# A recurrent graph kernel: gates and updates as a pinned pipeline of half batches, the first half batch's gate products inside the last product chain, and one set of sums in another order

## The chip, the cores and the metric

The kernel runs on one core of one Trainium2 chip. The metric is the device time of an execution in microseconds (us); lower is better. Quoted times are medians of several executions. Every execution in this study was in the fast state, at a granted TensorE clock of 0.995 to 0.999 of full speed.

## The reference, cut to what matters

A batch of 16 graphs with 1024 nodes and 128 features shares one dense 1024 x 1024 matrix `adj`. The first layer is one product with `adj`, a residual and a layer norm. The second is a gated recurrence of five steps, in which both the "in" and the "out" matrix are `adj`:

```python
def step(h, _):
    m_in = jnp.einsum('nm,bmd->bnd', in_matrix, h)      # in_matrix == out_matrix == adj
    m_out = jnp.einsum('nm,bmd->bnd', out_matrix, h)
    av = jnp.concatenate([m_in, m_out], axis=-1)
    u3 = h @ u3_w.T + u3_b
    z = jax.nn.sigmoid(av @ w3_w.T + w3_b + u3)
    r = jax.nn.sigmoid(av @ w4_w.T + w4_b + u3)
    hv = jnp.tanh(av @ w5_w.T + w5_b + (r * h @ u5_w.T + u5_b))
    h = (1.0 - z) * h + z * hv
    return (h, None)
# layer 0: x = layernorm(x + adj @ (x @ weight) + bias)
# layer 1: x = layernorm(x + five steps of the above on x)
```

## The kernel before

The product with `adj` (an **aggregation**) takes four batches at once, a group, so there are 4 aggregations for the first layer and 4 x 5 = 20 for the second. In this text they are numbered 0 to 23, and a **step** is the stretch from one aggregation's start to the next one's: aggregation, then gates and updates of four batches. In 12 of the steps, here called closing steps (10 to 13, 15 to 18 and 20 to 23), the group before is normalised and stored as well; steps without that are called plain. An aggregation is a two-level Strassen-Winograd scheme: outer products 1 to 7, each of them built from seven inner products, called P1 to P7 here. They run as four chains, for the outer pairs (1,2), (3), (6,7) and (5,4). Inputs of the inner products are sums that VectorE makes: four "outer sums" (`tsum`, 1.22 us each) and "inner sums" (`inner`). The inner products share three banks of PSUM:

```python
        after = {
            1: lambda: nc.scalar.copy(fb, fa),            # P1 is copied into pb, on which P6, P7, P4 accumulate
            5: lambda: nc.scalar.copy(x22, fc),
            6: lambda: nc.scalar.copy(x12, fb),
            2: lambda: nc.scalar.copy(x11, fa),
            7: lambda: nc.vector.tensor_add(x22, fb, x22),  # reads pb; P4 may not write it before
            3: lambda: nc.vector.tensor_add(x12, fc, x12),
            4: lambda: nc.scalar.copy(x21, fb),
        }
        bank_of = {1: pa, 2: pa, 5: pc, 3: pc, 6: pb, 7: pb, 4: pb}
        for a in order:
            for hook in hooks.get(a, ()):
                hook()
            for o, n in enumerate(ns):
                for c in range(2):
                    product = nc.tensor.matmul(bank_of[a][:, ts(o, QT)], chunk(a, o, c), left[n][a][:, c, :], ...)
            ...
            with tc.high_priority(), behind:
                after[a]()
            drain(3 if len(ns) == 2 else 1)      # a few activations of a deferred normalisation
```

The gates work on half batches of 512 columns, eight to a step. Each takes five products: the first one by `u3`, then `w4` (for r) and `w3` (for z), then the two update products by `w5` and `u5`. The first product is used twice: `w4` accumulates on top of it in its own bank, and ScalarE copies it to a second bank (`seeded`) for `w3`. I call that copy the seed copy.

```python
    def gate_first(tag, k, h):
        pu = bank(f"pu_{tag}_{k}_{h}")                    # one of three rotating banks, taken as they come free
        pin(nc.tensor.matmul(pu, w_t["u3"], hid[:, k, ts(h, HALF)], start=True, stop=True, ...))
        pin(nc.scalar.copy(seeded[h], pu))
        pus[h] = pu

    def gate_rest(tag, k, h):
        ...
        pin(nc.tensor.matmul(pu, w_t["w4"], agg[:, k, cols], start=False, stop=True, ...))
        pin(nc.scalar.activation(rh[:, cols], pu, AF.Sigmoid, bias=br))
        pin(nc.vector.tensor_mul(rh[:, cols], rh[:, cols], hid[:, k, cols]))
        pin(nc.tensor.matmul(pz, w_t["w3"], agg[:, k, cols], start=False, stop=True, ...))
        pin(nc.scalar.activation(z[:, cols], pz, AF.Sigmoid, bias=bz))
...
            hooks[54][4] = [call(gate_half, tag, 0, 0)]   # ahead of P4 of the last chain
            aggregate(tag, rows, hooks, s > 0)
            gate_half(tag, 0, 1)
            for k in range(QUAD):
                if k < QUAD - 1:
                    gates(tag, k + 1)
                update(tag, k, not last)
```

`pin` pins nothing in the steps: it calls `keep_in_program_order` only near the end of the program. What is not pinned is ordered by the framework's scheduler when the program is built. `keep_in_program_order` keeps an instruction behind whatever the program text has pinned before it on the same engine.

## Time and profile before

| | before |
|---|---|
| time, median of the 3 executions known before the prediction (lowest to highest) | 1797.4 us (1795.1 to 1798.0) |
| span of the profiled execution, clock | 1796.2 us, 0.998 |
| TensorE busy, by the page | 99% |
| time lost between passes (defined below) | 36.8 us |

Most of what follows uses one measure. **Lost time** is the distance from one matmul's start to the next one's, less the median distance of that shape (0.118, 0.216 and 0.429 us for 128, 256 and 512 columns), summed. It is worked out from the trace's matmul records, and it is needed because matmul ends are modelled: a busy share of 99% still hides 2% of lost time. In a timeline the same thing is read from neighbouring starts: four passes of 256 columns should be followed 0.86 us later by the next group.

In the lines quoted here, `pb<-s,inner` is a product into tile `pb` from operands `s` and `inner`; `x4` is the number of instructions merged in one line; `[0.58 <-DVE hvs L233]` means that the engine was idle for 0.58 us just before and that a VectorE (DVE) instruction of line 233 on tile `hvs` ended it. The timelines have the start and the duration in us in the first two columns. The gate tiles r and z appear as `tsum`, because they lie in the same memory.

### The profile page before, as it was taken

The page shows a single profiled execution, that of the slowest core. Times are in us where ns is not written, and L with a number is a line of the kernel's source. Part 1 is how long each engine was busy: PE and PEld are TensorE (multiplying, and loading weights), DVE is VectorE, ACT ScalarE, POOL GpSimd, SP SyncE. Part 2 cuts the span into 40 slices and gives each one's busy share as a digit, 9 for nine tenths or more (in the row PEclk, how much of TensorE's full clock was granted, in tenths as well). Part 3 has the DMA queues.
Part 4 walks back from the last instruction along what each step waited for, and adds up shares of the span by engine and source line. Part 5 has one row for each costly group of instructions (what it writes and reads, how often), then busy time and mean ns, then how long its engine had stood idle before and what let it go on. Part 6 is the DMA issues. An engine that isn't in the chain of part 4 may idle for free.

```text
span 1796.2 us, 19819 instructions
## 1 busy us (share of the span) xinstructions
PE 1775.3 (99%) x6709; PEld 1259.2 (70%) x6709; DVE 1309.0 (73%) x2280; ACT 789.3 (44%) x1418; POOL 94.5 (5%) x142
## 2 busy tenths in 40 slices
PE   8999999999999999999999999999999999999998
PEld 7788884857668576675857657586775857667584
DVE  7977786676857857777776857777777576867777
ACT  2345555243343434435354343534435254453536
POOL 0112220000000000000000000000000000000004
PEclk9999999999999999999999999999999999999999
DMA  6233353240513415252342414334243231513232
GB/s 225 71 118 127 109 144 74 66 95 23 117 36 90 110 36 117 60 128 59 95 103 85 105 38 115 74 85 112 58 107 105 48 81 48 118 36 94 68 74 94
DMA packets 404212, 159.23 MB, mean 89 GB/s; under 512 B 388241, under 2 KB 389137, under 8 KB 404113
## 3 DMA queue, kind: packets, MB, share of 16 engines
q1 hardware_dynamic: 403248, 154.84, 33.8%
q10 hardware_dynamic: 864, 3.15, 0.5%
q8 instruction: 53, 0.87, 0.2%
q14 instruction: 47, 0.38, 0.1%
HBM read 92.93 MB, written 65.01 MB: 88 GB/s over the span
## 4 chain that ended last, share of the span: by engine, by line
PE 89%; DVE 6%; issue 1%; DMA 1%; POOL 1%; ACT 1%; SPq 0%; DVEq 0%; POOLq 0%
PE pb L364 22%; PE pc L364 12%; PE pa L364 12%; PE pu L467 8%; PE pu L456 8%; PE seeded L472 7%; PE ph L485 7%; PE ph L484 7%; PE pc_x L364 2%; PE pa_x L364 2%; PE seeded L433 1%; POOL rstd L247 1%; DVE tsum L324 1%; DMA rows<-in_x_dram 1%; ACT ypad L252 1%
## 5 line engine op out<-in xcount | busy, mean ns | idle before, releaser
L364 PE MATMUL pb<-e,inner 128*128 128x256 f32 x864 | 206.8, 380 | 2.8 <-ACT pb L350 2.6
L364 PEld LDWEIGHTS pb<-e,inner 128*128 128x128 f32 x864 | 167.3, 194 | 23.4 <-ACT pb L350 4.7
L471 DVE TENSOR_TENSOR tsum<-tsum,hid 128x512 f32<-128x512 f32 x160 | 107.0, 684 | 96.5 <-ACT tsum L470 96.3
L501 DVE TENSOR_TENSOR tsum<-tsum,hid 128x512 f32<-128x512 f32 x158 | 108.5, 687 | 93.4 <-ACT tsum L495 93.3
L495 ACT ACTIVATE tsum<-ph,bh 128x512 f32<-128x512 f32 x158 | 108.5, 687 | 147.4 <-PE ph L485 147.3
L467 PE MATMUL pu<-agg,w_t 128*128 128x512 f32 x320 | 167.6, 610 | 0.7 <-DVE agg L416 0.7
L485 PE MATMUL ph<-tsum,u_t 128*128 128x512 f32 x320 | 163.6, 593 | 0.1
L484 PE MATMUL ph<-agg,w_t 128*128 128x512 f32 x320 | 163.7, 593 | 0.0
L472 PE MATMUL seeded<-agg,w_t 128*128 128x512 f32 x320 | 162.0, 592 | 0.0
L364 PE MATMUL pb<-s,inner 128*128 128x256 f32 x576 | 150.7, 384 | 0.5 <-DVE agg L354 0.5
L456 PE MATMUL pu<-hid,u_t 128*128 128x512 f32 x320 | 150.9, 593 | 0.0
L364 PE MATMUL pb<-a,inner 128*128 128x256 f32 x576 | 144.9, 380 | 0.7 <-DVE first L354 0.7
L364 PE MATMUL pc<-e,inner 128*128 128x256 f32 x560 | 134.6, 380 | 0.0
L470 ACT ACTIVATE tsum<-pu,br 128x512 f32<-128x512 f32 x160 | 108.7, 686 | 54.7 <-PE pu L467 47.5
L364 PEld LDWEIGHTS pb<-s,inner 128*128 128x128 f32 x576 | 109.1, 194 | 23.3 <-DVE rows L354 8.1
L364 PEld LDWEIGHTS pb<-a,inner 128*128 128x128 f32 x576 | 111.5, 195 | 15.6 <-DVE first L354 2.0
L475 ACT ACTIVATE tsum<-seeded,bz 128x512 f32<-128x512 f32 x160 | 109.2, 686 | 23.1 <-PE seeded L472 19.4
L364 PEld LDWEIGHTS pc<-e,inner 128*128 128x128 f32 x560 | 108.8, 195 | 12.7 <-issue 1.4
L503 DVE TENSOR_TENSOR hid<-hid,tsum 128x512 f32<-128x512 f32 x158 | 109.2, 691 | 10.3
L485 PEld LDWEIGHTS ph<-tsum,u_t 128*128 128x128 f32 x320 | 60.8, 190 | 76.9 <-issue 72.1
L472 PEld LDWEIGHTS seeded<-agg,w_t 128*128 128x128 f32 x320 | 60.9, 190 | 76.4 <-issue 76.4
L484 PEld LDWEIGHTS ph<-agg,w_t 128*128 128x128 f32 x320 | 60.6, 190 | 75.3 <-issue 70.4
(180 smaller groups left out, 2842.0 us busy)
## 6 DMA issues: line engine op xcount, KB each, us to landing
turned<-ypad SPq DMA_DIRECT2D x48, 512.0 KB, 3.8
rows<-turned SPq DMA_DIRECT2D x192, 128.0 KB, 2.9
hvs<-saved SPq DMA_DIRECT2D x24, 512.0 KB, 4.1
rows<-saved SPq DMA_DIRECT2D x20, 512.0 KB, 4.9
hid<-hidden SPq DMA_DIRECT2D x64, 128.0 KB, 3.6
turned<-ypad SPq DMA_DIRECT2D x32, 256.0 KB, 2.9
rows<-turned SPq DMA_DIRECT2D x128, 64.0 KB, 2.1
hid<-in_x_dram SPq DMA_DIRECT2D x12, 512.0 KB, 4.6
```

What stands on the lines that cost most here:

```text
L364: product = nc.tensor.matmul(bank_of[a][:, ts(o, QT)], chunk(a, o, c), left[n][a][:, c, :], start=(a in (1, 5) and o == 0 and c == 0), sto ...
L456: pin(nc.tensor.matmul(pu, w_t["u3"], hid[:, k, ts(h, HALF)], start=True, stop=True, skip_group_check=True))
L467: pin(nc.tensor.matmul(pu, w_t["w4"], agg[:, k, cols], start=False, stop=True, skip_group_check=True))
L470: pin(nc.scalar.activation(rh[:, cols], pu, AF.Sigmoid, bias=br))
L471: pin(nc.vector.tensor_mul(rh[:, cols], rh[:, cols], hid[:, k, cols]))
L472: pin(nc.tensor.matmul(pz, w_t["w3"], agg[:, k, cols], start=False, stop=True, skip_group_check=True))
L475: pin(nc.scalar.activation(z[:, cols], pz, AF.Sigmoid, bias=bz))
L484: pin(nc.tensor.matmul(ph, w_t["w5"], agg[:, k, cols], start=True, stop=False))
L485: pin(nc.tensor.matmul(ph, w_t["u5"], rh_of[k % 2][:, cols], start=False, stop=True))
L495: pin(nc.scalar.activation(hv, ph, AF.Tanh, bias=bh))
L501: pinned(nc.vector.tensor_sub(hv, hv, hid[:, k, cols]))
L503: pinned(nc.vector.tensor_add(hid[:, k, cols], hid[:, k, cols], hv))
```

## The change

The intent is to take TensorE's small recurring waits out of the steps. Nothing is computed differently; only order, banks and pins change.

1. The last chain's order is P1, P5, P6, P2, P7, **half of P3, the w4 product of half batch 0, P4, its w3 product, the other half of P3**, all pinned.
2. Gates and updates run as a **pipeline of half batches**, in which the next first product, an update and a gate alternate. All its products are pinned and the three gate banks are assigned by number.
3. In the second chain's wake, the inner sums of outer products 6 and 7 come before two of the four **outer sums**.
4. The first gate products of the next step, and of the **next group**, are pinned ahead of its aggregation.

The diff, cut to its core:

```diff
-    def outer_sums(src, early=True, late=True):
+    def outer_sums(src, early=True, late=True, pinned=False):
 ...
         if turned:
-            last_sum = sums_of(src, (3,), True)
-            last_outer = outer_sums(src)
-        sums_of(src, (6, 7))
-        with tc.issue_after(last_sum.ins) if turned else nullcontext():
+            sums_of(src, (3,), True)
+            outer = outer_sums(src, True, False, True)
+        inner_67 = sums_of(src, (6, 7), turned)
+        with tc.issue_after(inner_67.ins) if turned else nullcontext():
+            if turned:
+                outer_sums(src, False)
 ...
+                    if item != a or (ns == (5, 4) and a == 4):
+                        tc.keep_in_program_order(product)
 ...
-            order=(1, 5, 6, 2, 7, 4, 3),
+            order=(1, 5, 6, 2, 7, (3, (0,)), 4, (3, (1,))),
 ...
+    in_order = tc.keep_in_program_order
+    UNITS = [(k, h if k < 3 else 1 - h) for k in range(QUAD) for h in range(2)]
+    part_of = [0, 1, 2]
 ...
-            hooks[54][4] = [call(gate_half, tag, 0, 0)]
+            if q == s == 0:
+                hooks[54][3, (0,)] = [call(gates_begin, tag, 3)]
+            hooks[54][4] = [call(gate_r, 0, False)]
+            hooks[54][3, (1,)] = [call(gate_z, 0)]
             aggregate(tag, rows, hooks, s > 0)
 ...
-            gate_half(tag, 0, 1)
+            with behind_closing():
+                gate_rh(0)
+            if not end:
+                gate_seed(2)
+            gate_r(1)
+            gate_z(1)
 ...
-            for k in range(QUAD):
-                if k < QUAD - 1:
-                    gates(tag, k + 1)
-                ...
-                update(tag, k, not last)
+            for u in range(3, 8):
+                gate_first(tag, u, (u - 3) % 3)
+                step_update(u - 3, (u - 2) % 3)
+                gate_r(u - 1)
+                gate_z(u - 1)
+            step_update(5, 2)
+            gate_r(7)
+            gate_z(7)
+            step_update(6, 0)
+            step_update(7, 1)
+            part_of.insert(0, part_of.pop())
+            then = f"{q}_{s + 1}" if not last else f"{q + 1}_0"
+            gates_begin(then, 2 if q == NQ - 1 and s == STEPS - 2 else 3)
```

Here `u` numbers the half batches 0 to 7. `gate_rh` multiplies r by h on VectorE and `gate_seed` is the seed copy.

## The prediction

> **What bounds the kernel now.** I read the page first, then the chain of waits in order of time, then the waits, then the timeline of one step. The page's first part gives the order of the engines:
>
> ```profile
> PE 1775.3 (99%) x6709; PEld 1259.2 (70%) x6709; DVE 1309.0 (73%) x2280; ACT 789.3 (44%) x1418; POOL 94.5 (5%) x142
> ```
>
> TensorE has almost no idle time; VectorE has a quarter of the span to spare, ScalarE more than half. But matmul ends are modelled, so 99% is not yet proof. The chain of waits gives a better clock, because it lists issue slots without overlap. It repeats once per recurrent step (20 steps: four groups of four batches, five steps each):
>
> ```profile
> 310.98 2.58 PE pu L456 x6
> 313.56 1.73 PE pa L364 x8
> ...
> 388.25 2.57 PE pu L456 x6
> 390.82 1.73 PE pa L364 x8
> ...
> 465.54 2.58 PE pu L456 x6
> ...
> 542.71 2.58 PE pu L456 x6
> ```
>
> The reader is to see three things. Eight passes of a 128x256 product take 1.73 us, so 0.216 each; six passes of a 128x512 product take 2.58, so 0.430 each. The distance between repeats is 77.27, 77.29 and 77.17 us. A step has 4704/24 = 196 small passes (the groups of the page, over 4 + 20 aggregations) and 5 x 320/20 = 80 wide ones, thus 196 x 0.216 + 80 x 0.430 = 42.3 + 34.4 = 76.7 us. So a step wastes about 0.6 us of 77.2. **There is very little to win.**
>
> To count it over the whole run I took the start-to-start distance of every pair of neighbouring matmul records and subtracted the median of its shape (0.118, 0.216, 0.429 us). All 6709 passes at their medians make 1750 us, the lost time is 37 us, and after the last matmul comes a tail of 8 us (normalise and store). Of the 37 us, 21 lie before the recurrent steps (loading, weight sums, first layer with its projections), 0.5 in the last transposes and 15 in the 20 steps. Only those 15 us can be reached by this change.
>
> Where the 15 us sit shows in the timeline, at the end of an aggregation:
>
> ```profile
> 431.36 1.03 PE L364 MATMUL pc<-e,tsum 128*128 128x256 f32 x4
> 431.63 0.69 DVE L354 TENSOR_TENSOR rows<-pb,rows 128x512 f32<-128x512 f32 x1 [4.46 <-PE pb L364]
> 432.37 0.74 PEld L364 LDWEIGHTS pb<-s,inner 128*128 128x128 f32 x4 [0.39 <-DVE rows L354]
> ...
> 434.21 1.03 PE L364 MATMUL pc<-e,tsum 128*128 128x256 f32 x4
> 434.41 0.58 ACT L356 COPY rows<-pb 128x512 f32<-128x512 f32 x1 [4.00 <-PE pb L364]
> ...
> 435.03 0.69 DVE L416 TENSOR_TENSOR agg<-rows 128x512 f32<-128x512 f32 x1 [2.71 <-ACT rows L356]
> 435.07 1.88 PE L467 MATMUL pu<-agg,w_t 128*128 128x512 f32 x4
> ...
> 435.77 0.35 PEld L467 LDWEIGHTS pu<-agg,w_t 128*128 128x128 f32 x2 [0.51 <-DVE agg L416]
> ```
>
> P4 (pb<-s) has to wait until VectorE has read P7 out of pb. The scheduler had already put half of P3 (0.86 us) between; it is too short, and about 0.26 us go. The second place is the gates:
>
> ```profile
> 438.51 1.02 PE L456 MATMUL pu<-hid,u_t 128*128 128x512 f32 x2
> ...
> 439.62 0.57 ACT L459 COPY seeded<-pu 128x512 f32<-128x512 f32 x1 [0.23 <-PE pu L456]
> 440.24 1.13 PE L467 MATMUL pu<-agg,w_t 128*128 128x512 f32 x2
> ```
>
> ```profile
> PEld pu L467 <- ACT seeded L459: 38.4, 64, 0.7
> PEld pb L364 <- DVE rows L354: 8.1, 17, 0.8
> ```
>
> The product L467 accumulates into the bank that ScalarE is still copying. The weight load waits 38.4 us in total, but most of that is hidden under the running product: in TensorE's starts it is 0.07 to 0.10 us each time, 0.24 to 0.31 us a step.
>
> **What the Trainium skill says.** "Perfetto Trace Analysis", Identifying the Most-Contended Engine: matmul busy time is no good measure of the distance to the roofline, since pipelined instructions overlap. Agreed: a 128x512 pass is shown with 593 ns and starts every 430. "TensorE: Matmul & The Clock Gate", Back-to-back issue gap: about 518 cycles for 512 columns at 2.4 GHz, 216 ns. For float32 this trace has 430 ns a pass and two passes a product, so I use the trace. "PSUM — Partial Sum Buffer", PSUM bank collisions: two engines on one bank have to be kept apart with a semaphore. That is why L467 waits for the copy of its own bank, as above. "Perfetto Trace Analysis", Matmuls: independent groups should rotate through banks so that evacuation overlaps; that is the idea of this change, though the three gate banks rotate already.
>
> **The change, part by part.** It adds no arithmetic: same products, copies, sums, transfers. It alters order only.
>
> (1) *Gate products among P3 and P4.* After P7 TensorE now runs half of P3, the w4 product of half batch 0 (0.86 us), then P4, the w3 product, the rest of P3. P4 starts 1.72 us after P7 instead of 0.86 + 0.26. VectorE's add was through 0.96 us after P3's start (431.36 to 432.32), so the wait is covered. By the lost-time count this gap took 4.5 us in the steps. After P4 come 1.72 us of products before the w4 product of half batch 1, which needs P4's copy and an add: 434.21 to 435.72, 1.51 us, release at 435.77. It just fits; at the very end of the program, where nothing stood between, this same dependence cost 0.93 us, and the change should recover that too. Gain 5 us.
>
> (2) *Pipeline of half batches.* Each round is first product, two update products, w4, w3 = 5 x 0.86 = 4.3 us. Seed copies now have at least two update products (1.72 us) before the bank is accumulated into; they need 0.2 + 0.57. The lost 0.24 to 0.31 us a step should vanish: 5.4 us over all. Per round ScalarE has 0.57 + 3 x 0.69 = 2.64 us and VectorE 4 x 0.69 + half a turn of 1.25 = 3.4 us, both under 4.3. A bank is rewritten 1.72 us after the product whose result is read (0.2 + 0.69), so 0.8 us to spare.
>
> (3) *Sums reordered.* Inner sums for P6/P7 come before two outer sums of 1.22 us that only the last chain needs. The wait here was small: 0.65 us in all. But the old order used the first gate products as filling in the middle of the aggregation (L467 and L472 at 407.92, 1.72 us), and that filling is gone. So the reordering pays for (1) and I count 0.5 us.
>
> (4) *Group boundaries.* First gate products of the next group are pinned before its aggregation (2.58 us of filling), which should hide the 0.5 us wait before P4 of the first chain: 3 x 0.5 = 1.5 us.
>
> Sum of gains: 5 + 5.4 + 0.5 + 1.5 = 12.4 us.
>
> **Rivals.** *A: pinned order brings its own waits.* Two places are tight. At the tail of a step the last update needs r times h of half batch 7, made only 3.44 us earlier: sigmoid 0.89, then VectorE behind an update (2.07) and perhaps a turn (1.25). If the turn goes first, TensorE waits about 0.9 us, x19 = 17 us, and the change would be slower by 5 us (1802). Against it: in the old trace the scheduler slips independent sums between dependent ones, so the multiply likely goes before. I give this one in six. Second, in the 12 steps with a deferred normalisation ScalarE does eight extra activations (3.2 us) just where sigmoids free the banks; I take 0.2 to 0.3 us each, 3 us. *B: nothing changes because the gaps move.* A wait hidden now by free scheduling may reappear elsewhere, with TensorE pinned; this would give 1795 to 1799. *C: VectorE becomes the bound.* At 73% it has room over a step, and its backlog at the step's start (last update added at 396.06, TensorE's last update product over at 388.08) should shrink, since the second-last batch's updates come 1.7 us earlier. Against C then. *D: a transfer.* The turned rows arrive by 402.4, just before P3's chain; they should come earlier, so they don't bind.
>
> **Range and chances.** 12.4 gained, 3 lost to the normalisation, 1 for small new waits: 8.4 us, so 1797.4 - 8.4 = 1789. If all 15 us of the steps went, 1782; with the tail wait, 1802; with half of the gain, 1793. I take 1782 to 1799. Faster by 2% would be 1761, below what is left even with no loss in the steps (1750 + 21 + 0.5 + 8 = 1780): practically impossible. Slower by 2% (1833) needs 1.8 us lost a step: unlikely.
>
> **What would show it.** In the changed trace: step distance 76.7 to 77.0 in the chain of waits; the pair L467 waiting on the seed copy gone; P4 of the last chain without a wait; no wait on the multiply by h before the u5 product at a step's tail (if there is one of 0.5 us or more, rival A holds); TensorE's first 250 us unchanged. Wrong would be a time over 1799 or a step distance over 77.3.

## The result

| | before | after |
|---|---|---|
| time, median of 6 executions | 1797.6 us (1795.1 to 1798.2) | 1790.7 us (1788.7 to 1791.9) |
| span of the profiled execution, clock | 1796.2 us, 0.998 | 1790.1 us, 0.996 |
| lost time | 36.8 us | 31.3 us |

The ratio of the fast executions is 0.9963, with a 95% interval of 0.9950 to 0.9976: 0.4% faster, which counts as the same at a threshold of 2%. Ratios in this document are the mean time of one kernel's fast runs over that of the other's in the same rounds, so not quite the ratio of the medians quoted. The later groups of runs were on other chips, so across groups ratios are to be compared, not microseconds.

The new page's first part:

```profile
PE 1768.5 (99%) x6709; PEld 1267.6 (71%) x6709; DVE 1309.0 (73%) x2280; ACT 789.9 (44%) x1418; POOL 94.3 (5%) x142
```

And the chain of waits over three plain steps (start, us in the chain, engine, tile, line, count):

```profile
391.43 2.58 PE pu L476 x6
...
468.06 2.58 PE pu L476 x6
...
544.70 2.58 PE pu L476 x6
```

The engines do the same work as before: VectorE's busy time is even equal to the tenth. The distance between repeats is now 76.63 and 76.64 us, against 77.29 and 77.17 before. That is the prediction's sum of a step's products, 76.7 us, so plain steps lose nothing that can be measured.

The end of an aggregation, in the timeline (TensorE's rows and VectorE's addition of P7):

```profile
432.69 1.03 PE L377 MATMUL pc<-e,tsum 128*128 128x256 f32 x4
432.96 0.69 DVE L365 TENSOR_TENSOR rows<-pb,rows 128x512 f32<-128x512 f32 x1 [4.46 <-PE pb L377]
...
433.55 1.02 PE L494 MATMUL pu<-agg,w_t 128*128 128x512 f32 x2
...
434.41 1.03 PE L377 MATMUL pb<-s,inner 128*128 128x256 f32 x4
...
437.00 1.03 PE L377 MATMUL pc<-e,tsum 128*128 128x256 f32 x4
```

P4 (`pb<-s`, 434.41) starts 0.86 us after the w4 product at 433.55, without a wait; VectorE's add of P7 had been through at 433.65. The other half of P3 follows at 437.00, 2.59 us and thus three groups of products after P4's start, so nothing is lost in between either.

In the list of waits (total us, count, longest us), the longest waits that TensorE's weight loads have left on gates and updates:

```profile
PEld ph L517 <- ACT tsum L497: 8.5, 11, 0.8
```

They occur 11 times and are released by ScalarE's sigmoid; where they come from is shown with close_late below. The 38.4 us of loads waiting for the seed copy are gone from the list but for 2.0 us. A larger sum has come up: loads of the `u5` product (L518) wait 71 times for the multiply by h (L504), 17.3 us in all and 0.5 at most, where it was 8 times and 2.9 us. These waits lie under running products and delay no start in the plain steps.

Now the whole span, cut by the starts of the aggregations, from the two traces:

| stretch | before, us | after, us | difference |
|---|---|---|---|
| to the start of aggregation 1 | 65.34 | 66.24 | +0.90 |
| aggregation 1 | 55.45 | 56.60 | +1.15 |
| aggregation 2 | 51.90 | 54.95 | +3.05 |
| aggregation 3 | 51.57 | 51.38 | -0.19 |
| 4, with the first step's gates | 89.14 | 88.04 | -1.10 |
| 5 to 22 | 1390.51 | 1382.01 | -8.50 |
| 23 and the end | 92.26 | 90.90 | -1.36 |
| sum | 1796.16 | 1790.11 | -6.06 |

So the steps gained 11.0 us, more than the prediction's net 8.4, and the first layer, which was expected to stay as it was, lost 4.9 in these two profiled executions. The experiments ask what the parts are worth and where the 4.9 us come from.

### The profile page after: what moved, and what is told of

The parts are those of the page before. It is cut to its first block, busy times and chain, and to the rows that moved or that the text cites. A ratio compares the mean times of both kernels' runs of the same rounds, so it can differ in the third digit from the quotient of the medians.

```text
span 1790.1 us, 19915 instructions
## 1 busy us (share of the span) xinstructions
PE 1768.5 (99%) x6709; PEld 1267.6 (71%) x6709; DVE 1309.0 (73%) x2280; ACT 789.9 (44%) x1418; POOL 94.3 (5%) x142
## 4 chain that ended last, share of the span: by engine, by line
PE 93%; DVE 3%; POOL 1%; ACT 1%; issue 1%; DMA 0%; SPq 0%; DVEq 0%; POOLq 0%
PE pb L377 23%; PE pa L377 13%; PE pc L377 13%; PE ph L517 8%; PE pu L476 8%; PE pu L494 8%; PE seeded L509 8%; PE ph L518 8%; PE pa_x L377 2%; PE pc_x L377 2%; PE seeded L451 1%; POOL rstd L252 1%; ACT ypad L257 0%; DMA rows<-in_x_dram 0%; DVE stats L246 0%
## 5 line engine op out<-in xcount | busy, mean ns | idle before, releaser
L533 DVE TENSOR_TENSOR tsum<-tsum,hid 128x512 f32<-128x512 f32 x158 | 108.8, 689 | 107.7 <-ACT tsum L528 107.6
L517 PE MATMUL ph<-agg,w_t 128*128 128x512 f32 x320 | 164.7, 596 | 0.0
L509 PE MATMUL seeded<-agg,w_t 128*128 128x512 f32 x320 | 163.5, 592 | 0.0
L518 PE MATMUL ph<-tsum,u_t 128*128 128x512 f32 x320 | 163.5, 592 | 0.0
L476 PE MATMUL pu<-hid,u_t 128*128 128x512 f32 x320 | 157.1, 592 | 0.0
L504 DVE TENSOR_TENSOR tsum<-tsum,hid 128x512 f32<-128x512 f32 x160 | 110.4, 690 | 46.4 <-ACT tsum L497 46.4
L517 PEld LDWEIGHTS ph<-agg,w_t 128*128 128x128 f32 x320 | 59.8, 190 | 78.2 <-issue 69.0
L518 PEld LDWEIGHTS ph<-tsum,u_t 128*128 128x128 f32 x320 | 61.0, 190 | 76.4 <-issue 57.5
L476 PEld LDWEIGHTS pu<-hid,u_t 128*128 128x128 f32 x320 | 61.0, 191 | 73.4 <-issue 72.3
L534 DVE TENSOR_TENSOR tsum<-tsum 128x512 f32<-128x512 f32 x158 | 109.2, 691 | 5.0
```

What stands on the lines that cost most here:

```text
L476: in_order(nc.tensor.matmul(pu, w_t["u3"], hid[:, k, ts(h, HALF)], start=True, stop=True, skip_group_check=True))
L509: in_order(nc.tensor.matmul(pz, w_t["w3"], agg[:, k, cols], start=False, stop=True, skip_group_check=True))
L517: in_order(nc.tensor.matmul(ph, w_t["w5"], agg[:, k, cols], start=True, stop=False))
L518: in_order(nc.tensor.matmul(ph, w_t["u5"], rh_of[k % 2][:, cols], start=False, stop=True))
L533: pinned(nc.vector.tensor_sub(hv, hv, hid[:, k, cols]))
L534: pinned(nc.vector.tensor_mul(hv, hv, z_of[k % 2][:, cols]))
```

## The experiments

Twelve runs, in three groups on three chips. All results were correct. Unless said otherwise an edit is against the changed kernel.

### The first layer: the weights prepared earlier (weights_early)

At 121 us, in aggregation 1, the second layer's weights are summed by VectorE and transposed by TensorE, all pinned, just ahead of P4 of the last chain. Before, P4 was not pinned. The timelines of the two kernels there, before first:

```profile
117.86 0.70 PE L364 MATMUL pb<-s,inner 128*128 128x256 f32 x2
...
118.40 0.27 PE L231 MATMUL pt_w<-ident,hvs 128*128 128x128 f32 x1
...
118.51 0.60 PE L364 MATMUL pb<-s,inner 128*128 128x256 f32 x2
```

```profile
121.59 0.33 PE L236 MATMUL pt_w<-ident,hvs 128*128 128x128 f32 x1 [0.58 <-DVE hvs L233]
...
121.97 1.03 PE L377 MATMUL pb<-s,inner 128*128 128x256 f32 x4
```

Before, a transpose (`pt_w`, 118.40) stands between two halves of a P4 product (117.86 and 118.51), and TensorE waits for none of the transposes. In the changed kernel P4 (`pb<-s`, 121.97) is pinned too and comes behind all transposes, one of which waits 0.58 us for a sum on VectorE. The theory: the pin costs some 3 us here and, by delaying the projections that follow, in aggregation 2. The edit puts the weights ahead of P7 instead, where a product is there to run:

```diff
         if q == 1:
-            hooks[54][4] = [layer1_weights]
+            hooks[54][7].append(layer1_weights)
```

> The changed kernel is slower than the old one before the recurrent steps: its third first-layer aggregation takes 54.95 us against 51.90, lost time 5.06 against 1.66. Theory: P4 is now pinned behind the transposes of the second layer's weights, which stand ahead of P4 in this one aggregation and wait for VectorE; so P4, the next chain and the projections come late (a wait of 1.97 us, then half the TensorE rate for 3 us). Edit: the weights' transposes stand ahead of P7 instead. Expected if so: that aggregation back at 51.9 to 52.5 us, the start of the fifth aggregation about 3 us earlier than in the changed kernel, whole time 2 to 3.5 us less (1787 to 1788.5). Rival: noise of the profiled run (loads landing later, clock) - then that aggregation stays near 55 us and the time stays at 1790.6.

Measured: 1787.2 us (4 runs), ratio 0.9933 (0.9916 to 0.9950). The changed kernel was not run in this group; its ratio in the first was 0.9963, with an interval that touches this one, so the trace has to decide. Aggregations 1 and 2 took 55.50 + 51.42 = 106.9 us, as before the change (107.35), against 110.05 in a repeat of the changed kernel. The first part of the theory holds: the pinned P4 behind the weights cost about 3 us. How the delay gets from 121 us to the wait below I did not follow link by link; that it goes with the edit is what the run shows.

The changed kernel was also run again (after_again) to see how constant the rest is.

> The changed kernel again, on the same chip as the next three. Expected 1789 to 1791.5, 0.35 to 0.4% below the old kernel; whether the third first-layer aggregation takes 53.3 us or 55 us should go with a second or third stretch of half TensorE clock of 3.4 us before 150 us in the record.

Measured: 1791.9 us (5 runs), ratio 0.9959 (0.9947 to 0.9972). Aggregation 2 took 53.35 us, not 54.95. The missing 1.6 us are a clock effect. In the first trace of the changed kernel, TensorE waits here for a bias copy, and just afterwards its clock is halved. The timeline's row, then the stretches by engine (window, length, busy us and instructions of PE, PEld, DVE, ACT and POOL, granted clock, DMA share, GB/s), after and then before:

```profile
140.67 2.15 PE L451 MATMUL seeded<-w_sb,agg 128*128 128x128 f32 x12 [1.81 <-ACT seeded L448]
```

```profile
141.70:145.10 3.40, 3.40 (x14) 3.12 (x13) 2.01 (x7) 0.25 (x1) 0.53 (x3) 0.50 0.38 154
```

```profile
141.70:145.10 3.40, 3.40 (x23) 3.01 (x23) 3.39 (x6) 3.36 (x9) 2.53 (x2) 1.00 0.47 152
```

The Trainium skill ("TensorE: Matmul & The Clock Gate", Part 1: The HAM clock gate) describes a free-running window of 3413 ns and a half-rate clock after an idle one. The trace agrees with the length and the rate: every slow stretch before the last matmul is 3.413 us (once twice that) at 0.5. Each costs about half of that, 1.7 us. There is one at about 90 us in 12 of the 14 traces, mostly after a wait of 2.75 us at 86 us, and one at 12 us in five of them. The one at 141.7 us follows the wait of the row above, 1.97 us by the lost-time count; of ten traces with that wait this is the only one with the slow stretch.

Why only this one? Within each trace the slow stretches start whole multiples of 3.413 us apart (here at 11.968, 90.475 and 141.675 us, thus 23 and 15 windows). If the lost time is summed by the windows of that grid, each of the 17 stretches before the last matmul follows a window in which TensorE lost 2.07 us or more; windows at full clock without one after them lost at most 2.08. The wait of 1.97 us lies whole in the window 138.26 to 141.67 here. In the repeat a window's end cuts it and 1.83 us are left. In no_boundary and close_late even the wait of 2.75 us is cut, the larger part is 1.77 and 1.69 us, and the stretch at 90 us is missing. So not a whole idle window was needed here but a loss of about 2.1 us within one, and where the grid happens to lie decides whether a wait of 2 to 3 us costs another 1.7. This is read from the traces; no run set out to test it.

This would also explain why the changed kernel's six executions fall in two clusters, 1788.7 to 1789.7 us at a clock of 0.998 and 1791.6 to 1791.9 at 0.996 to 0.997; that is an inference, as only profiled executions show the stretches.

### The tail of a step: is rival A real? (tail_late)

The prediction's rival A was that the turn of the rows (1.25 us) would run before the multiply by h that the last update product needs. In the changed kernel it does not:

```profile
465.01 0.68 DVE L504 TENSOR_TENSOR tsum<-tsum,hid 128x512 f32<-128x512 f32 x1
...
466.33 1.25 DVE L555 STREAM_TRANSPOSE ypad<-hid 128x1024 f32<-128x1024 f32 x1
```

The multiply of half batch 7 (L504) starts at 465.01, between two update operations of which one needs the other's result (L534 and L535), and the turn (L555) waits until 466.33. Was that luck worth what the rival said? The edit forces the multiply behind the turn:

```diff
-            gate_r(7)
+            gate_r(7, False)
+            in_order(gate_rh(7))
             gate_z(7)
```

> Rival A of the prediction: VectorE's multiply by h of half batch 7 is pinned behind the turn of batch 2 (1.25 us). In the changed kernel it slipped in between two dependent operations of an update. Expected if the margin is as tight as worked out (release needed about 1 us before the u5 product would start): a wait of 0.7 to 1.0 us before the last u5 product in each of the 19 full steps, 13 to 19 us in all, 1804 to 1810. If there is more slack than worked out: no wait, 1790 to 1792.

```profile
465.70 1.25 DVE L555 STREAM_TRANSPOSE ypad<-hid 128x1024 f32<-128x1024 f32 x1
...
466.87 0.65 DVE L504 TENSOR_TENSOR tsum<-tsum,hid 128x512 f32<-128x512 f32 x1
...
467.57 1.13 PE L518 MATMUL ph<-tsum,u_t 128*128 128x512 f32 x2 [0.59 <-DVE tsum L504]
```

Measured: 1805.2 us (4 runs), ratio 1.0039 (1.0024 to 1.0054). In the lost-time count the last `u5` product (L518) costs 0.85 us in 16 steps, the first four of each group, and 0.42 us at the three boundaries between groups: 14.9 us in all. So the rival's sum was right in size, though not for all 19 steps; what kept it away was one instruction slipped between two dependent ones.

### The filling: P3 and P4 without the gate products (no_fill)

```diff
-            hooks[54][4] = [call(gate_r, 0, False)]
-            hooks[54][3, (1,)] = [call(gate_z, 0)]
             aggregate(tag, rows, hooks, s > 0)
 ...
+            gate_r(0, False)
+            gate_z(0)
             with behind_closing():
                 gate_rh(0)
```

> Undoes the filling of part 1 alone: the w4 and w3 products of half batch 0 stand behind the last chain instead of among P3 and P4; all else as in the changed kernel. Expected: the wait before P4 of the last chain returns, 0.26 us in each of 20 steps, about 5 us (1795 to 1796.5), 0.4 to 0.9 us in the steps with a deferred normalisation; no wait for the sum that half batch 1 needs, as two products stand ahead of it. If the filling was worth nothing: 1790 to 1791.

Measured: 1793.7 us (6 runs), ratio 0.9970 (0.9958 to 0.9982). The wait before P4 is back, 0.26 us in every step. But the waits of the 12 closing steps (next experiment) are gone, because the gates now run 1.72 us later with respect to the normalising activations. So over aggregations 5 to 22 the loss is 4.6 us against 3.1, and in aggregation 23 with the end 2.3 against 1.4. The filling takes out the wait that it was meant to, but gives more than half of it back in another place; its net worth is 1.5 + 0.9, about 2.5 us by the count. The two intervals of the ratio (0.9958 to 0.9982, and 0.9950 to 0.9976 for the changed kernel) overlap, so the times alone don't show it. My expectation had the first and not the second.

### The closing steps (close_late)

Twelve steps close a batch of the group before: eight normalising activations on ScalarE (L257), released three items of the chain after their statistics. They stand in ScalarE's queue ahead of the sigmoid that frees a gate bank:

```profile
745.10 0.87 ACT L257 ACTIVATE hvs<-hvs,shift,rstd 128x128 f32<-128x128 f32 x2
...
746.38 0.68 ACT L497 ACTIVATE tsum<-pu,br 128x512 f32<-128x512 f32 x1
...
747.12 1.13 PE L517 MATMUL ph<-agg,w_t 128*128 128x512 f32 x2
```

The `w5` product (L517) wants the bank of half batch 1's gate, which the sigmoid at 746.38 is reading. The sigmoid stands behind normalising activations (the two at 745.10 are the last of them in front of it). TensorE loses 0.24 us here, and so in six of the closing steps. In the other six (13, 18, 20 to 23) P4's copy stands behind such activations too, and the w4 product of half batch 1 waits for the sum that needs the copy:

```profile
PEld pu L494 <- DVE agg L434: 2.1, 6, 0.5
```

There the w4 product loses 0.18 to 0.34 us, and but for step 23 the `w5` product another 0.16. Over aggregations 5 to 22 the two places cost 1.1 and 2.3 us. The edit releases the activations three items later during the steps:

```diff
-    def drain(n, age=3):
+    patience = [3]
+
+    def drain(n, age=None):
+        age = patience[0] if age is None else age
 ...
+    patience[0] = 6
     for q in range(NQ):
```

> The changed kernel, with the eight activations of a deferred normalisation released six slots after it instead of three, so that they fall into the next step's first chain and not beside the first sigmoids. Theory: the 0.23 to 0.34 us lost in each of the 11 or 12 steps with a deferred normalisation are the w5 product waiting for the sigmoid of half batch 1 to free its bank behind those activations: all go, 3 us in all, steps at 76.64 us. Rival: they then delay the copies of the first chain, and the same 0.2 to 0.4 us shows there.

Measured: 1787.5 us (4 runs), ratio 0.9946 (0.9931 to 0.9960), against 0.9964 for no_boundary in the same group. The closing steps take 76.64 us like the plain ones, except one with 0.07 and one with 0.29 us lost. So the 3 us that the prediction charged to the normalisation are there, in that place, and they can be had.

### The group boundary (no_boundary)

Part 4 of the change puts the next group's first gate products ahead of its aggregation, and the wait of 0.5 us before P4 of its first chain is gone. Did the filling do it? In the changed kernel TensorE's order at a boundary is:

```profile
621.17 1.89 PE L377 MATMUL pa<-a,rows 128*128 128x256 f32 x8
622.90 1.88 PE L476 MATMUL pu<-hid,u_t 128*128 128x512 f32 x4
```

The gate products (L476) are not ahead of the aggregation: the scheduler put them behind P1 of the first chain. The edit leaves them in the last chain, as in the very first step:

```diff
-            if q == s == 0:
+            if s == 0:
                 hooks[54][3, (0,)] = [call(gates_begin, tag, 3)]
 ...
-            gates_begin(then, 2 if q == NQ - 1 and s == STEPS - 2 else 3)
+            if not last:
+                gates_begin(then, 2 if q == NQ - 1 and s == STEPS - 2 else 3)
```

> Undoes part 4 alone: the first gate products of a group of batches stand at the end of its first aggregation, as in the group that comes first, and not ahead of it. Expected: the old wait of about 0.5 us before P4 of the first chain returns in the first aggregation of groups 2 to 4, 1.5 us in all (within noise of the changed kernel's time; the trace decides). Rival: the update pipeline has already taken VectorE's backlog away, then no wait there and part 4 was worth nothing.

```profile
617.71 1.89 PE L377 MATMUL pa<-a,rows 128*128 128x256 f32 x8
619.44 1.89 PE L377 MATMUL pc<-e,inner 128*128 128x256 f32 x8
```

Measured: 1790.0 us (5 runs), ratio 0.9964 (0.9951 to 0.9977), as the changed kernel. Aggregations 9, 14 and 19, which open a group, lose nothing without the filling either. Only aggregation 15 loses 0.45 us more. So part 4 is worth nothing measurable, and the wait at the boundary was removed by something else. The kernels without the pipeline, below, still lose 0.48 to 0.50 us there. That leaves part 2.

### The sums (old_sums)

The prediction counted 0.5 us for the new order of the sums, with the remark that it pays for the removed filling. The edit restores the old order:

```diff
         if turned:
-            sums_of(src, (3,), True)
-            outer = outer_sums(src, True, False, True)
-        inner_67 = sums_of(src, (6, 7), turned)
-        with tc.issue_after(inner_67.ins) if turned else nullcontext():
-            if turned:
-                outer_sums(src, False)
+            last_sum = sums_of(src, (3,), True)
+            outer = outer_sums(src)
+        sums_of(src, (6, 7))
+        with tc.issue_after(last_sum.ins) if turned else nullcontext():
             nc.vector.tensor_add(agg[:, 0:2, :HALF], two(first[:, 0]), two(first[:, 1]))
```

> Undoes part 3 alone: all four outer sums ahead of the inner sums of P6 and P7. In the changed kernel the inner sums are ready 1.3 to 1.4 us before P5 and P6 start; the two late outer sums take 2.35 us. Theory (reordering pays for the removed filling): a wait of about 0.9 to 1.1 us before P5 or P6 of the third chain in the 16 steps with turned rows, 14 to 18 us, 1804 to 1809. Rival (the reordering is worth the 0.65 us that the old kernel lost there): 1790 to 1792.

```profile
487.11 1.22 DVE L327 TENSOR_TENSOR tsum<-tsum,rows 128x1024 f32<-128x1024 f32 x1
...
488.47 1.11 PE L377 MATMUL pa<-s,tsum 128*128 128x256 f32 x4 [0.25 <-DVE tsum L327]
...
490.97 1.14 PE L377 MATMUL pb<-s,inner 128*128 128x256 f32 x4 [0.53 <-DVE agg L365]
```

Measured: 1809.1 us (4 runs), ratio 1.0057 (1.0042 to 1.0072). P1 of the third chain (488.47) waits for an outer sum (L327), which runs behind one that only the last chain needs, 0.50 us by the lost-time count. P4 of the second chain (490.97) waits for an addition of P7 (L365) that stands in VectorE's queue behind the last outer sum and a turn, 0.80 us. With 0.12 us behind them that makes 1.4 us in the plain steps; ten of the 18 steps 5 to 22 lose this or more in addition, five lose 0.5 and the first steps of groups nothing. Together it is 18 us. The size is as expected, the place only in part. The reordering is therefore the largest single term of the change, when it is undone alone.

### Part 1 alone, and with part 3 (p34_only, p34_sums, p34_sums2)

These start from the kernel before. The first takes over the new P3 and P4 with the pins (in the chain function as in the change) and the gate products between them:

```diff
-            order=(1, 5, 6, 2, 7, 4, 3),
+            order=(1, 5, 6, 2, 7, (3, (0,)), 4, (3, (1,))),
 ...
-            hooks[54][4] = [call(gate_half, tag, 0, 0)]
+            hooks[54][3, (0,)] = [call(gate_first, tag, 0, 0)]
+            hooks[54][4] = [call(gate_rest_r, tag, 0, 0, tc.keep_in_program_order)]
+            hooks[54][3, (1,)] = [call(gate_rest_z, tag, 0, 0, tc.keep_in_program_order)]
```

> The old kernel with part 1 alone: P3 split around a pinned P4, the w4 and w3 products of half batch 0 pinned among them; old order of sums, old batch-wise gates left to the scheduler. Theory: the 0.26 us wait before P4 goes (4.5 us over the steps, 0.9 us at the very end), but the two products no longer fill the middle of the aggregation, where the late sums now show: 1.0 to 1.5 us before the second and third chains in the 16 steps with turned rows, as undoing the new sum order in the changed kernel did (1.4 us a step). Expected 5 to 20 us slower than the old kernel. Rival: the scheduler finds other filling (products of half batch 2), then 3 to 6 us faster than the old kernel.

Measured: 1816.8 us (4 runs), ratio 1.0112 (1.0095 to 1.0129). The waits of old_sums are all there, 0.50 and 0.80 us, and in some steps 1.35 instead of 0.50, together with 0.24 to 0.37 us of waits for seed copies. Part 1 alone costs 20 us. Some 3 of them are the first layer's, which this kernel and the next two share with the changed one (aggregation 2 takes 53.3 us in all three, 51.9 before).

The second adds the sums' new order as the diff of the change has it.

> The old kernel with parts 1 and 3: as the run before, and inner sums of P6 and P7 ahead of the late outer sums. Theory: the waits in the middle go, the one before P4 is gone, the waits on the seed copies (0.24 to 0.31 us a step, 5.4 us) stay as in the old kernel: 4 to 6 us faster than the old kernel, with 0.2 to 0.4 us lost a step. The difference to the changed kernel's 0.0 us in a plain step is then part 2. Rival: without the pipeline VectorE is 1.7 us later at the step's start, and waits of 0.3 us or more stay before the second or third chain.

Measured: 1815.4 us, ratio 1.0105 (1.0090 to 1.0120); I had expected a gain. The plain steps did as expected: 76.90 us, with only the seed copies' 0.24 lost. But six closing steps (10 to 12 and 15 to 17) lose 3.6 to 4.0 us each:

```profile
742.51 0.69 DVE L485 TENSOR_TENSOR tsum<-tsum,hid 128x512 f32<-128x512 f32 x1 [3.54 <-ACT tsum L484]
...
743.21 0.66 DVE L356 TENSOR_TENSOR rows<-pb,rows 128x512 f32<-128x512 f32 x1
...
743.92 1.14 PE L368 MATMUL pb<-s,inner 128*128 128x256 f32 x4 [0.27 <-DVE rows L356]
```

The multiply by h (L485) was issued to VectorE early, because its product now comes early. It waits for its sigmoid, VectorE is idle for 3.54 us, and the last statistics of the normalisation and the addition of P7 (L356) wait behind it, as the queue keeps its order. P4 waits for the addition (0.54 us by the lost-time count), and through P4's copy so does the next w4 product (1.22 us). The Trainium skill says in one sentence that ScalarE and VectorE are strict FIFO ("TensorE: Matmul & The Clock Gate", Architectural detail); this run shows what one small instruction in front can cost. The changed kernel has the multiply apart (`gate_rh` under `behind_closing`), for which I had seen no reason.

The third therefore moves the multiply behind the chain and the normalisation's statistics:

```diff
-            hooks[54][4] = [call(gate_rest_r, tag, 0, 0, tc.keep_in_program_order)]
+            hooks[54][4] = [call(gate_rest_r, tag, 0, 0, tc.keep_in_program_order, False)]
 ...
+            with (tc.issue_after(closed[0].ins) if closed[0] else nullcontext()):
+                gate_rh(0, 0)
             gate_half(tag, 0, 1)
```

> The old kernel with parts 1 and 3 once more, mended: in the run before it the multiply by h of half batch 0 stood in VectorE's queue ahead of the end of a deferred normalisation and waited there for a sigmoid, so that the add before P4 came late (3.6 us in each of 7 steps). Here the multiply is put behind the chain and behind the normalisation, as the change does. Theory: plain steps keep 0.24 us (seed copies), steps with a normalisation fall from 3.6 us to 0.3 to 0.6; whole time 1793 to 1797, 2 to 4 us faster than the old kernel; what is left to the changed kernel is part 2. Rival: those steps keep over 1 us, because the eight activations hit the batch-wise gates harder.

Measured: 1807.2 us (4 runs), ratio 1.0048 (1.0034 to 1.0061): better, and still a miss. The six closing steps fall from 3.6 us or more to 1.8 to 2.1 us (one 3.1), so the multiply at the head of the queue cost some 1.8 us in each. What is left in them:

```profile
744.73 1.12 PE L466 MATMUL pu<-hid,u_t 128*128 128x512 f32 x2 [0.78 <-ACT tsum L484]
...
751.34 1.13 PE L509 MATMUL ph<-agg,w_t 128*128 128x512 f32 x2 [0.32 <-ACT tsum L484]
```

The scheduler put an unpinned first product (L466) right before P4, into the bank that the sigmoid L484 was still reading (as in p34_sums): 1.04 us by the lost-time count. The `w5` product (L509) waits for a bank in the same way, 0.58 us. Three banks rotate here as well, but which product takes which bank next, and when, is left to the scheduler. The group boundary loses its 0.49 us and the seed copies their 0.24 us in every step. So part 1 needs part 2: what the pipeline brings is not only the seed copies' 5 us but an order in which early gate products don't run into busy banks. This is argued from the two traces; no run added part 2 alone.

### The pieces together (best, best6)

`best` combines weights_early and close_late and puts the last batch's half batches in the order in which the end of the program wants them. In the changed kernel the half that GpSimd starts with gets its z last, and the last transposes wait for GpSimd:

```profile
1778.27 1.21 PE L757 MATMUL pt_end<-ident,first 128*128 128x128 f32 x8 [0.62 <-POOL first L743]
```

```diff
-                    for u in (2 * k, 2 * k + 1):
+                    for u in sorted((2 * k, 2 * k + 1), key=lambda u: UNITS[u][1]):
```

> The changed kernel with three mends: weights' transposes ahead of P7 (3.1 us in its single run), normalising activations released later in the steps (3 us), and at the very end the two half batches of the last batch in the order in which the closing products want them. In the changed kernel 0.88 us are lost before the first closing product, by theory because GpSimd starts with half 0, whose z comes last. Expected: 1784 to 1786, the 0.88 us gone or under 0.3; the steps without loss; 0.7% below the old kernel. Rival for the end: the wait only moves to the second half (0.4 us or more remain).

Measured: 1785.0 us (5 runs), ratio 0.9919 (0.9905 to 0.9933). Aggregation 23 loses 0.81 us in place of 1.38: the 0.88 us wait is gone, but the one of 0.51 us that the kernel before has (the transposes waiting for the last VectorE product) is back. The gain at the end is thus 0.6, not the whole 0.9. In this trace the wait at 86 us is 4.5 us long, with a slow stretch of 6.8 us after it; why, I don't know.

`best6` is the same with the late release also in the first layer (`patience = [6]` from the start), because the wait at 86 us has the same form: ScalarE waits for GpSimd's shift (2.88 us idle in the changed kernel's trace), and the copy that P6 needs stands behind.

> As the run before, with the later release in the first layer too. In the changed kernel ScalarE waits 2.88 us at 85.5 us for GpSimd's shift with a copy that TensorE needs behind it, TensorE idles 2.6 us, and 3.4 us of half TensorE clock follow: 4 us together. Theory: with the activations released three slots later that wait and the half clock after it go: 3 to 4.5 us less, 1780 to 1782. Rival: the activations then hold up other copies or projections later in the first layer, and less than 1.5 us is won.

Measured: 1781.1 us (4 runs), ratio 0.9899 (0.9885 to 0.9912). Aggregation 1 loses 0.93 us instead of 6.1, and the slow clock stretch at 90 us is not there. Two new waits of 0.87 and 0.81 us appear in aggregations 2 and 3. Lost time over the program is 20.2 us, against 31.3 in the changed kernel. This version beats both kernels: 1.0% faster than before, where the change itself gives 0.4%.

## Why the prediction was right or wrong

**The time was right:** 1789 predicted, 1790.7 measured, well inside 1782 to 1799, and within 2% as said. It was right in part by luck, because errors cancel. By the prediction's own steps:

- *There is very little to win; only the steps' 15 us can be reached.* The first half held. The steps gained 11.0 us of the 15. The second half failed: the change also reached the first layer, by 4.9 us in the wrong direction.
- *Part 1, 5 us.* The wait before P4 is gone from every step that had it. By the count that was 12 of the steps 5 to 22, 0.26 us each and 3.2 in all; the prediction's 4.5 us, for all 20 steps, is reached only with two waits of 0.44 us before P4 of the second chain. But undoing the filling costs only 2.5 us net, since it also moves the gates towards the normalising activations. And alone, part 1 makes the kernel 1.1% slower. The sum treated it as separable, and it isn't.
- *Part 2, 5.4 us.* Confirmed by the trace: in the plain steps no seed-copy wait is left in TensorE's starts (5.2 us over aggregations 5 to 22 before). The prediction put the wait itself down to a rule on banks; it needs none, as the w4 product adds to the very values that the copy has yet to read. No run undid part 2 alone. p34_sums2, which has parts 1 and 3 without it, shows that it also removes the boundary's wait and the bank collisions of early gate products.
- *Part 3, 0.5 us.* As a difference from the kernel before, the small wait of 0.65 us is indeed gone. As the worth of the part, the number was far too small: undone alone it costs 18 us. The prediction had the mechanism (it pays for the removed filling) and no size for it.
- *Part 4, 1.5 us.* The wait did vanish, but the step's reason failed: no_boundary shows the same without the filling. Pinning the products ahead of the aggregation doesn't even put them there.
- *Rival A.* It did not happen, for the reason given: the multiply slipped between dependent updates. tail_late shows its size was right: 0.85 us against "about 0.9", in 16 steps and not 19. The prediction's 1802 for this case left out its own 3 + 1 us of other losses; measured were 7 us more than before by the ratio.
- *Normalisation, 3 us.* Right in size: 0.24 to 0.5 us in each closing step, 3.07 us over aggregations 5 to 22, and close_late removes it. The place was right in part: banks that a late sigmoid frees, but in six steps also P4's copy and its sum, the dependence of which the prediction said that it just fits.
- *Rivals B, C and D.* In the plain steps no gap moved, VectorE did not become the bound, and no transfer binds.
- *The end of the program.* Of the 0.93 us dependence 0.19 is left. The 0.5 us wait for the last VectorE product turned into one of 0.88 us for GpSimd.
- *"TensorE's first 250 us unchanged".* This is the step that failed. I had looked for what the change does in the recurrent steps. But the new order of P3 and P4 is in the function that all aggregations use, and its pin applies to every last chain. In the first layer pinned weight transposes stand in front of it. About 3 us are shown to come from that order by weights_early. The 1.6 us more in aggregation 2 are a half-clock stretch that one of two profiles of this kernel has. The +0.9 us before aggregation 1 go with another such stretch: aggregation 0 began 0.74 us earlier but took 55.43 us in place of 53.78, with a stretch at 12 us in it. The five traces that have one at 12 us take 55.4 to 55.9 us there, the nine others 53.8 to 54.4, so no run shows it as a cost of the order.

The step distance was predicted as 76.7 to 77.0 and is 76.64 in plain steps, 76.88 to 77.00 in those closing ones that have the same work.

## What to carry to other kernels

Pin the order of the bounding engine only together with its banks and with the queues of the engines that feed it: the same pinned products cost 20 us alone, 19 with the new order of VectorE's sums and 9 with the multiply moved back as well, and gained only with the banks fixed too; one multiply at the head of an in-order queue held TensorE up by 1.8 us in a step. When a pin goes into a shared function, look at every caller: it also drags along whatever pinned work stands before it elsewhere. And count lost time between starts instead of busy shares; here it located gaps of 0.24 us, and several of them went when a deferred job was released a little later or earlier.

## What the Trainium skill lacked or had wrong

- "TensorE: Matmul & The Clock Gate", Why this matters for your kernels, asks for no TensorE idle gaps beyond about 3 us. Here a stretch of 3.413 us at half clock followed a wait of 2.75 us in ten of twelve traces, and a wait of 1.97 us in one of ten. What told them apart was the lost time within one window of 3.413 us: 2.07 us or more with a stretch after it, at most 2.08 without. So gaps under 3 us can be enough.
- The same page, Back-to-back issue gap, has no time for float32. A pass of 512 columns starts every 0.429 us here, one of 256 columns every 0.216 us and one of 128 every 0.118 us, and a float32 product shows as two such passes.
- The same page says that ScalarE and VectorE are strict FIFO, but nothing on what this costs. One multiply waiting for its sigmoid held VectorE's queue for 3.54 us, and moving it back saved TensorE 1.8 us in that step.
- "Perfetto Trace Analysis", Matmuls, advises independent groups to rotate through banks. Rotation alone was not enough: with three rotating banks and a free order a product waited 1.04 us for its bank in p34_sums2; with the order and the bank numbers fixed, plain steps lose nothing.
- No page says what a fixed program order does to other work that is fixed too: P4 pinned behind the weight transposes cost about 3 us.
